# Graph layers on one core: the order of the first loads, earlier searches, first logits inside layer 0, and one product for q and k

## The chip, the cores and the metric

The kernel runs on one core of a Trainium2 chip. The time is the device time of one execution in microseconds; for the kernel before it is the median of 3 runs, 1922.41 us (1921.39 to 1923.52). The profile is of one more execution, of 1922.35 us, with a span of 1920.6 us from its first instruction to its last.

Engines are named as in the profile: PE is TensorE (PEld its weight loads), DVE is VectorE, ACT is ScalarE, POOL is GpSimd, SP is SyncE. An fp32 matmul appears as two PE instructions. [...] DMAs are issued by SP, ACT and POOL.

## What is computed

x has 3327 rows of 256. Layer 0 is a graph attention over a sparse adjacency (3327 x 3327, a few ones in a row) with a gated update; layer 1 makes two propagation steps with a top-p attention over all rows. Each has a residual and a layer norm. Cut to what matters here:

```python
# layer 0
Wh = h @ W
src, dst = Wh @ a[:F], Wh @ a[F:]
e = leaky_relu(src + dst.T, 0.2)
att = softmax(where(adj > 0, e, NEG_INF), axis=1)
h_prime = att @ Wh
gi = h_prime @ w_ih.T + b_ih ; gh = h @ w_hh.T + b_hh
... # r, z, n of a gated unit, then layernorm
# layer 1, for each of two steps
q = Xa @ W1.T @ W2.T
k = Xa @ W3.T
probs = softmax(q @ k.T)
A = probs, kept to the largest that make up 0.9 of a row, normalised
Xf = R @ Xf          # R: (S + identity) over its row sums
Xa = A @ Xa
Z = Z + Xf @ U1[n].T + Xa @ U2[n].T
```

In this program S is the adjacency of layer 0, so that R needs the same neighbour lists. A row without neighbours has the mean of Wh as h_prime; in the table whx this mean is row N.

## The kernel before

**Tiles.** Rows go in 26 tiles of 128 (the last has 127). `HALF` is 1664, the columns of 13 tiles, and `LC` is 416, a quarter of it. kT keeps the keys of the first half on partitions 0 to 63 and those of the second on 64 to 127, and qT has the queries twice, on both halves, so that a product with 64 partitions can take either half of the columns.

**Set-up.** `Shared.__init__` (L514) loads W3, W1 and W2, makes wq = W1 W2 on PE in a pool of its own ("once", released afterwards), and wk; both are doubled in width to fill 128 columns. `Layer0.__init__` (L626) then loads x in pieces on SP (`load_rows`, L635), and on ACT's queue W, its transpose WT, a, the biases, whh and wih. The bias is split into three bf16 parts by DVE (L659 to L661), each of which ACT's queue moves into a row of `bias16` (L662), through one buffer. The three adjacency buffers `ad` are cleared in their borders by POOL (L668, L669).

**Layer 0.** `run` (L978) writes the order out by hand for PE, ACT, DVE and POOL.
- `weights` (L705) multiplies WT by a into two more columns of W.
- `project(t)` (L718): transposes x (L723), multiplies by W (L728), copies into a tile w (L732, three buffers), and ACT issues the write of w to the table whx in DRAM (L735, through `move_rows`, L91). POOL keeps the two added columns in `ds`.
- `column_sums` (L739), and `totals` (L741): column mean of Wh and the largest dst, written to whx as row N; it also fills the columns BOUND, SC and SC3 of `tell`.
- `neighbours(t)` (L783) finds the ones of adjacency tile t: four FIND_INDEX8 (L788), then sorting of the keys, and the load of tile t + 3 into the buffer that came free. It takes five calls.
- `tile(t)` (L804) is a generator with some 43 phases: membership (pst, y, mem, pe, ei), the row numbers (edge, L877), five indirect gathers from whx by POOL (L586, from phase 13), scores (L893 to L895), weights m (L906), acc (L912), gates (L920 to L941), update and layer norm (to L970), x1_rows written, and from phase 39 `Shared.qk` (L592): two transposes, four products (L607: two chunks for q, two for k), a copy to qT (L612) and one to kT (L615).

`advance` makes one phase: one call of the search (`find`), a new tile at every sixth phase, and one phase of each open tile. It is called once per projection from t = EARLY = 17 on; `find` alone from t = 11. After the last projection comes `totals`, then `advance` until all is done.

**Layer 1.** An item is one tile of one step. Per item: logits (`chunk`, L1106: a product of 64 x 416, L1112, and a copy, L1115) into one of two rows `l`; `list_1` (eights per group, L1128), `exp` (L1198), `list_2`, `exp_list`, `list_3`, `mask` (L1234) on DVE and ACT; `fetch` (gathers, L586, and membership tiles, L1271, on POOL); `propagate` (L1279); and `product`: 26 transposes (L1312), copies (L1314) and products (L1328). `run` (L1671) begins with the logits of items 0 and 1, all eight pairs, then the list of item 0, and in the loop makes the logits two items ahead. In step 0 `rest` makes q and k of the next step (`qk` again). At the change of step the last chunk of the first two items is made late (L1752 to L1755), since it needs the last tiles.

Of the kernel before, what the change touches and what calls it, by code (L numbers as in the profile page):

```python
# [16 lines left out]
P = 128  # L17
# [33 lines left out]

EVERY = 6

EARLY = 17
# [456 lines left out]
class Shared:  # L511


    def __init__(self, tc, ctx, W1T, W2T, W3T):  # L514
# [3 lines left out]
        dram = ctx.enter_context(tc.tile_pool(name="dram", bufs=1, space=bass.MemoryType.DRAM))  # L518
        self.ident = keep.tile([P, P], F32, name="ident")
# [3 lines left out]
        self.x1 = keep.tile([P, NT, D], F32, name="x1")  # L523

        self.wq = keep.tile([P, DC, 2 * DA], F32, name="wq")
        self.wk = keep.tile([P, DC, 2 * DA], F32, name="wk")
        for k in range(2):
            nc.scalar.dma_start(self.wk[:, :, k * DA : (k + 1) * DA], W3T.rearrange("(c p) d -> p c d", p=P))
        with ExitStack() as wctx:
            once = wctx.enter_context(tc.tile_pool(name="once", bufs=1))  # L530
            ps = wctx.enter_context(tc.tile_pool(name="onceps", bufs=1, space=PSUM))
            w1 = once.tile([P, DC, DA], F32, name="w1")
            nc.scalar.dma_start(w1, W1T.rearrange("(c p) d -> p c d", p=P))
            w2 = once.tile([DA, DA], F32, name="w2")
            nc.scalar.dma_start(w2, W2T)
            pt = ps.tile([DA, DC * P], F32, name="ptw")
            for c in range(DC):
                nc.tensor.transpose(pt[:, c * P : (c + 1) * P], w1[:, c, :], self.ident)
            w1t = once.tile([DA, DC * P], F32, name="w1t")
            nc.vector.tensor_copy(w1t, pt)  # L540
            pw = ps.tile([P, DC, DA], F32, name="pww")
            for c in range(DC):
                nc.tensor.matmul(pw[:, c, :], w1t[:, c * P : (c + 1) * P], w2, start=True, stop=True)
            for k in range(2):
                nc.vector.tensor_copy(self.wq[:, :, k * DA : (k + 1) * DA], pw)
# [36 lines left out]

    def gather(self, dst, table, t, parts=range(EB)):
# [8 lines left out]
    def qk(self, ps, work, n, t, src, apart=None):  # L592
# [12 lines left out]
        for k, w in enumerate((self.wq, self.wk)):  # L605
            for c in range(DC):
                nc.tensor.matmul(  # L607
                    pq[:, k * P : k * P + r], w[:, c, :], xt[:, c, :r], start=(c == 0), stop=(c == DC - 1)
                )
        if apart:  # L610
            yield
        nc.scalar.copy(self.qT[:, cols(t)], pq[:, :r])  # L612
        h = t * P // HALF
        on = slice(h * DA, (h + 1) * DA)
        nc.scalar.copy(self.kT[on, n, t * P - h * HALF : t * P - h * HALF + r], pq[on, P : P + r])  # L615
# [3 lines left out]
class Layer0:  # L619
# [3 lines left out]
    DST, SRC, ONE, WH = D, D + 1, D + 2, D + 3  # L623
    FIRST, ROW, SC, BOUND, SC3 = MAXDEG, MAXDEG + 1, MAXDEG + 2, MAXDEG + 3, MAXDEG + 4

    def __init__(self, sh, ctx, x, adj, W, WT, a, wihT, whhT, b_ih, b_hh):  # L626
# [7 lines left out]

        load_rows(nc, sh.x1, x, (0, 5, 15, NT - 1))  # L635
# [10 lines left out]
        nc.scalar.dma_start(bi, b_ih.unsqueeze(0))  # L646
        self.whh = keep.tile([P, DC, 3 * D], F32, name="whh")
        nc.scalar.dma_start(self.whh, whhT.rearrange("(c p) d -> p c d", p=P))
# [8 lines left out]
        for k in range(3):  # L657
            part = self.work.tile([1, 4 * D], BF16, tag="part", name=f"part{k}", bufs=1)
            nc.vector.tensor_copy(part, bias)  # L659
            if k < 2:  # L660
                nc.vector.tensor_tensor(bias, bias, part, ALU.subtract)  # L661
            nc.scalar.dma_start(self.bias[k : k + 1, :], part)  # L662
        self.xT = keep.tile([P, DC, N], F32, name="xT")

        self.ad = []
# [1179 lines left out]
```

## Time and profile before

| stage | from to (us) | what carries it |
|---|---|---|
| head: loads, projections | 0 to 87.1 (first gather from whx) | DMA share 0.20 to 1.10 by stretch, PE and ACT with gaps |
| layer 0, with searches | 87.1 to 319.0 | DVE 198.9, PE 185.8, POOL 173.3 of 231.9 us busy |
| layer 0, without | 319.0 to 436.3 (last kT copy) | PE 102.0, POOL 77.8, DVE 51.4 of 117.3 us busy |
| first items | 436.3 to 464.2 | logits of items 0 and 1, list, mask |
| step 0 | 464.2 to 1046 | 22.3 us per tile |
| change of step | 1046 to 1066 | late chunk, list, mask |
| step 1 and end | 1066 to 1920.6 | 21.8 us per tile, then the output |

```profile
PE 1683.6 (88%) x8229; PEld 1243.7 (65%) x8229; DVE 1368.4 (71%) x4291; ACT 902.3 (47%) x2006; POOL 1214.3 (63%) x1891
PE   4578889888999999999998899999999998997844
DVE  2778888434555555565553999999999987988771
PEclk9778999996999999999998899999999999999977
DMA  7666663212111111111111111111111121212110
```

The first line is the busy time of each engine with its share of the span and its instructions; the others divide the span into 40 equal slices (48 us each), a digit being the busy share in tenths. PEclk is the granted clock of PE. The profile's execution of 1922.35 us is within the runs' range, and its span is 1.75 us shorter than its time.

In the tables by stage each row has the stretch and its length, then for each engine the busy time and the number of instructions, then the granted clock, the DMA engines' busy share and GB/s. In a chain of waits each row has start, length and what was waited for: an engine with its line, a DMA, or "issue", in which nothing shown was waited for.

### The profile page before, as it was taken

To read this page: it belongs to the slowest core of one execution; us is meant where nothing else is said; L and a number is where in the kernel's file an instruction comes from. 1 tells how busy PE (TensorE), PEld (TensorE's weight loads), DVE (VectorE), ACT (ScalarE), POOL (GpSimd) and SP (SyncE) were. 2 spreads that over 40 slices of the span, in tenths; PEclk is the share of its full clock that TensorE was granted. 3 is DMA by queue.
4 is the path that set the end of the run, shared out by engine and by line. 5 is a ranking of instruction groups with operands and counts; after the bars stand their busy time and mean duration, and the time that the engine had idled before them with its cause. 6 is when DMAs were issued, how large, how long until landed. Compare 5 with 4: busy or idle time off the path is not lost.

```text
span 1920.6 us, 27507 instructions
## 1 busy us (share of the span) xinstructions
PE 1683.6 (88%) x8229; PEld 1243.7 (65%) x8229; DVE 1368.4 (71%) x4291; ACT 902.3 (47%) x2006; POOL 1214.3 (63%) x1891
## 2 busy tenths in 40 slices
PE   4578889888999999999998899999999998997844
PEld 3345556555777777777775677777777676676733
DVE  2778888434555555565553999999999987988771
ACT  1334445444555555555554455555555454334332
POOL 0277777846656666666664655666556574699993
PEclk9778999996999999999998899999999999999977
DMA  7666663212111111111111111111111121212110
GB/s 248 216 224 204 238 208 99 67 45 77 42 39 44 48 45 39 39 39 42 46 36 39 42 44 49 55 49 47 45 50 54 44 56 31 69 50 83 50 36 20
DMA packets 84192, 143.99 MB, mean 75 GB/s; under 512 B 15546, under 2 KB 57268, under 8 KB 84035
## 3 DMA queue, kind: packets, MB, share of 16 engines
q1 hardware_dynamic: 52272, 78.38, 12.4%
q0 software_dynamic: 20288, 53.27, 10.5%
q10 hardware_dynamic: 11474, 10.49, 1.7%
q8 instruction: 68, 1.11, 0.2%
q14 instruction: 90, 0.73, 0.1%
HBM read 117.84 MB, written 24.35 MB: 74 GB/s over the span
## 4 chain that ended last, share of the span: by engine, by line
PE 39%; DVE 36%; POOL 9%; DMA 5%; ACT 5%; issue 5%; ACTq 0%; POOLq 0%; DVEq 0%
PE pav L1328 17%; PE pl L1112 6%; DVE l L1248 6%; DVE cand L1128 5%; DVE p L1234 5%; DVE cand L1148 4%; PE pxf L1279 3%; PE pt L1312 3%; DVE lst L1146 3%; DMA g<-whx,edge 3%; PE pq L607 2%; POOL g L586 2%; DVE at L788 2%; PE prz L937 2%; PE pavh L1328 1%
## 5 line engine op out<-in xcount | busy, mean ns | idle before, releaser
L1328 PE MATMUL pav<-xa,at 128*128 128x256 f32 (+2 forms) x1352 | 329.8, 389 | 7.4 <-ACT at L1314 7.4
L1328 PE MATMUL pav<-x,at 128*128 128x256 f32 (+2 forms) x1352 | 327.6, 387 | 7.3 <-ACT at L1314 7.3
L1314 ACT COPY at<-pt 128x512 f32<-128x512 f32 (+2 forms) x364 | 191.8, 541 | 289.3 <-PE pt L1312 289.1
L1328 PEld LDWEIGHTS pav<-xa,at 128*128 128x128 f32 (+2 forms) x1352 | 245.6, 191 | 85.4 <-ACT at L1314 42.3
L1328 PEld LDWEIGHTS pav<-x,at 128*128 128x128 f32 (+2 forms) x1352 | 245.8, 191 | 72.2 <-ACT at L1314 29.6
L1128 DVE MAX8 cand<-l 128x8 f32<-128x208 f32 (+5 forms) x936 | 243.3, 336 | 53.6 <-ACT l L1115 53.6
L1115 ACT COPY l<-pl 128x416 f32<-128x416 f32 (+2 forms) x416 | 189.3, 506 | 194.3 <-PE pl L1112 194.3
L586 POOL DMA_INDIRECT g<-xf_rows,edge x130 | 135.8, 1045 | 166.6 <-PE pxf L1279 132.4
L586 POOL DMA_INDIRECT g<-x_rows,edge x130 | 136.2, 1047 | 129.6 <-PE ptq L599 96.8
L1112 PE MATMUL pl<-kT,qT 64*128 64x416 f32 (+1 forms) x832 | 214.2, 581 | 3.3 <-ACT l L1115 1.7
L1312 PE MATMUL pt<-ident,p 128*128 128x128 f32 (+1 forms) x1352 | 200.9, 275 | 15.6 <-DVE p L1234 15.6
L1312 PEld LDWEIGHTS pt<-ident,p 128*128 128x128 f32 (+1 forms) x1352 | 169.1, 144 | 51.9 <-PE pxf L1279 16.9
L1234 DVE SCALAR_TENSOR_TENSOR p<-l,t,p 128x3327 f32<-128x3327 f32 (+1 forms) x52 | 191.3, 3679 | 1.2 <-issue 0.2
L1218 DVE TENSOR_TENSOR_SCAN before<-e 128x40 f32<-128x40 f32 (+3 forms) x52 | 14.3, 275 | 230.5 <-ACT e L1211 230.5
L1198 ACT ACTIVATE p<-l,pay 128x1664 f32<-128x1664 f32 (+1 forms) x104 | 175.2, 1685 | 0.4 <-DVE pay L1190 0.4
L586 POOL DMA_INDIRECT g<-whx,edge x130 | 138.0, 1061 | 46.2 <-issue 30.5
L1271 POOL TENSOR_SCALAR m<-col,erow 128x128 f32<-128x128 f32 x260 | 153.1, 602 | 14.5 <-PE pxf L1279 8.1
L1279 PEld LDWEIGHTS pxf<-g,m 128*128 128x128 f32 (+1 forms) x520 | 99.7, 200 | 57.4 <-issue 39.9
L1279 PE MATMUL pxf<-g,m 128*128 128x256 f32 (+1 forms) x520 | 133.9, 407 | 3.1 <-DVE base L1426 3.1
L1146 DVE MAX8 lst<-cand 128x8 f32<-128x160 f32 (+3 forms) x364 | 114.5, 315 | 9.0
L788 DVE FIND_INDEX8 at<-ones,ad 128x8 uint32<-128x840 f32 (+1 forms) x104 | 106.4, 1026 | 0.0
L1112 PEld LDWEIGHTS pl<-kT,qT 64*128 64x128 f32 (+1 forms) x832 | 68.2, 190 | 45.2 <-issue 26.1
(372 smaller groups left out, 3007.8 us busy)
## 6 DMA issues: line engine op xcount, KB each, us to landing
ad<-in_adj_dram SPq DMA_DIRECT2D x25, 1248.0 KB, 6.4
ad<-in_adj_dram SPq DMA_DIRECT2D x25, 415.5 KB, 6.5
xf_rows<-xf SPq DMA_DIRECT2D x50, 128.0 KB, 1.7
xa_rows<-xa SPq DMA_DIRECT2D x50, 128.0 KB, 1.7
xfs<-xf_rows SPq DMA_DIRECT2D x50, 128.0 KB, 2.1
whx<-w ACTq DMA_DIRECT2D x25, 129.5 KB, 2.9
x_rows<-x ACTq DMA_DIRECT2D x25, 128.0 KB, 2.6
xf<-xf_rows SPq DMA_DIRECT2D x25, 128.0 KB, 2.0
```

The costliest lines, as they stand in the source:

```text
L586: self.nc.gpsimd.indirect_dma_start(out=dst[:, b, :], out_offset=None, in_=table[:, :], in_offset=bass.IndirectOffsetOnAxis(ap=self.edge[: ...
L1112: nc.tensor.matmul(pl[:r, :w], q[on], self.sh.kT[on, n, s : s + w], start=True, stop=True)
L1115: nc.scalar.copy(l[:r, h * HALF + s : h * HALF + s + w], pl[:r, :w])
L1128: self.nc.vector.max(cand[:r, g * 8 : g * 8 + 8], src[:r, g * group : min(N, (g + 1) * group)])
L1146: nc.vector.max(lst[:r, k : k + 8], cand[:r])
L1198: self.nc.scalar.activation(v.p[: v.r, on], v.l[: v.r, on], AF.Exp, bias=v.nmax[: v.r], accum_out=v.sums[: v.r, h : h + 1])
L1234: nc.vector.scalar_tensor_tensor(v.p[:r], v.l[:r, :N], v.t[:r], v.p[:r], ALU.is_ge, ALU.mult, accum_out=sA[:r])
L1271: nc.gpsimd.tensor_scalar(v.m[:, b, :], sh.col1, sh.erow[:, v.at, b : b + 1], None, ALU.is_equal)
L1279: nc.tensor.matmul(acc[:r, :D], v.m[:, b, :r], v.g[:, b, :], start=(b == 0), stop=(b == EB - 1))
L1312: nc.tensor.transpose(pt[: rows(j), j - j0, :r], v.p[:r, cols(j)], self.ident[:r, :r])
L1314: nc.scalar.copy(at[:, :full, :r], pt[:, :full, :r])
L1328: nc.tensor.matmul(v.acc[: v.r, :D], at[:k, j - 4 * g, : v.r], V[:k, j, :], start=(j == 0), stop=(j == NT - 1))
```

## The change

1. Order of the loads: x is loaded first, in pieces of 3, 6, 8 and 8 tiles, in `Shared`; W3, W1 and W2 after the biases; whh and wih only after projection 6. wq is made within the projections (at t = 8 and 10) from work tiles; no pool is released before layer 0. The bias parts have a buffer each and are moved by POOL's queue.
2. `EARLY` is 13 instead of 17, and the searches begin at t = 2 instead of 11. The tile w gets six buffers with the column of ones set once. The column sums are multiplied as they come, and `tell` is filled in two parts without the bound: BOUND goes, and each tile computes its own from src and the maximum (`most`).
3. The three adjacency buffers are shared arrays: once all searches are done, `first_logits` fills arrays 0 and 1 with the logits of step 0's first two tiles, chunk by chunk as their keys are finished (columns 0 to 3199), and the eights of item 0. Layer 1 uses these arrays as `l` and the third as one of its two p rows; it makes only the last 127 columns itself.
4. `qk`: the weights stand as k, q, k side by side, and one product of 128 columns gives both. qT is written by two copies (64 partitions each, one of them from the other half), kT by one.
5. At the change of step more columns of the two first items are made early.

```diff
-EARLY = 17
+EARLY = 13
+LATE = (NT - 1) * P - HALF
+FIRST_CHUNKS = [[(h, s, LC) for h in range(2)] for s in range(0, HALF - LC, LC)] + [
+    [(0, HALF - LC, LC), (1, HALF - LC, LATE - HALF + LC)]
+]
 class Shared:
+        load_rows(nc, self.x1, x, (0, 3, 9, 17, NT - 1))
...
+        self.arrays = [keep.tile([P, SEG * (SW + 8)], F32, name=f"array{k}") for k in range(3)]
+        self.cand = keep.tile([P, -(-N // GROUP[0]) * 8], F32, name="cand0")
+        self.wkqk = keep.tile([P, DC, 3 * DA], F32, name="wkqk")
...
+    def load_weights(self, work):
+        for k in (0, 2):
+            nc.scalar.dma_start(self.wkqk[:, :, k * DA : (k + 1) * DA], W3T.rearrange("(c p) d -> p c d", p=P))
...
     def qk(self, ps, work, n, t, src, apart=None):
-        for k, w in enumerate((self.wq, self.wk)):
-            for c in range(DC):
-                nc.tensor.matmul(
-                    pq[:, k * P : k * P + r], w[:, c, :], xt[:, c, :r], start=(c == 0), stop=(c == DC - 1)
-                )
+        h = t * P // HALF
+        on, other = slice(h * DA, (h + 1) * DA), slice((1 - h) * DA, (2 - h) * DA)
+        for c in range(DC):
+            nc.tensor.matmul(
+                pq[:, :r], self.wkqk[:, c, h * DA : h * DA + P], xt[:, c, :r], start=(c == 0), stop=(c == DC - 1)
+            )
-        nc.scalar.copy(self.qT[:, cols(t)], pq[:, :r])
+        for half in (on, other):
+            nc.scalar.copy(self.qT[half, cols(t)], pq[other, :r])
 class Layer0:
-            part = self.work.tile([1, 4 * D], BF16, tag="part", name=f"part{k}", bufs=1)
+            part = parts[:, k, :]
-            nc.scalar.dma_start(self.bias[k : k + 1, :], part)
+            nc.gpsimd.dma_start(self.bias[k : k + 1, :], part)
...
-            ad = keep.tile([P, SEG, SW + 8], F32, name=f"ad{k}")
+            ad = sh.arrays[k].rearrange("p (g c) -> p g c", g=SEG)
+        self.table = [keep.tile([P, self.WH], F32, name=f"table{k}") for k in range(6)]
...
+        most = self.small("most", f"most{t}", EB)
+        nc.gpsimd.tensor_scalar(most, src, self.dmax, None, ALU.add)
...
+        nc.vector.scalar_tensor_tensor(most, most, ALPHA, most, ALU.mult, ALU.max)
-        nc.vector.tensor_tensor(e, e, ei[:, :, self.BOUND], ALU.subtract)
+        nc.vector.tensor_tensor(e, e, most, ALU.subtract)
+    def first_logits(self):
+        while not self.searched:
+            yield
+        for chunks in FIRST_CHUNKS:
+            while self.done * P < chunks[-1][0] * HALF + chunks[-1][1] + chunks[-1][2]:
+                yield
+            for i in range(2):
...
+                    nc.tensor.matmul(
+                        pl[:, :w], sh.qT[half, cols(i)], sh.kT[half, 0, s : s + w], start=True, stop=True
+                    )
+                yield
+                for pl, (h, s, w) in zip(pls, chunks):
+                    nc.scalar.copy(sh.arrays[i][:, h * HALF + s : h * HALF + s + w], pl[:, :w])
+                yield
+                if i == 0:
...
+                            nc.vector.max(sh.cand[:, at : at + 8], sh.arrays[0][:, c : c + GROUP[0]])
+                    yield
     def run(self):
-        cuts = (0, 7, 14, 20, NT)
+        cuts = (0, 8, 16, 23, NT)
...
+                if t == 6:
+                    for w, src in zip((self.whh, self.wih), self.gates):
+                        nc.scalar.dma_start(w, src.rearrange("(c p) d -> p c d", p=P))
+                if t in (8, 10):
+                    next(qk_weights)
...
                 if t >= EARLY:
                     advance()
-                elif t >= EARLY - 6:
+                elif t >= 2:
                     find()
 class Layer1:
+            late, cut = [(1, LATE)], HALF + LATE
             for i in range(2):
                 self.item(i)
-                for pair in self.chunks():
-                    self.some_logits(i, pair)
+                self.some_logits(i, late)
             self.fetch(0)
-            self.list_1(0)
+            self.list_1(0, cut // GROUP[0] * GROUP[0], N)
...
-                        self.list_1(i + 1, 0, 9 * GROUP[1])
+                        done = [(cut - k * P) // GROUP[1] * GROUP[1] for k in (1, 0)]
+                        self.list_1(i + 1, 0, done[0])
+                        slot(6, self.some_logits, i + 1, [(1, LATE - P)], cut)
+                        slot(6, self.list_1, i + 1, *done)
```

## The prediction

> **What bounds the kernel now.** I read the page's row of slices, then the table by stage (busy time of each engine in a stretch, granted clock, DMA share, GB/s), and then the chain of waits inside each stage that the diff touches. Three stages matter, and each has a different limit.
>
> Table by stage, columns PE, PEld, DVE, ACT, POOL busy with counts, then clock, DMA share, GB/s:
>
> ```profile
> 24.00:30.00 6.00, 5.96 (x22) 4.83 (x23) 0.39 (x1) 0.90 (x3) 0.00 (x0) 1.00 1.04 412
> ...
> 36.00:42.00 6.00, 4.45 (x12) 3.48 (x13) 0.00 (x0) 2.32 (x7) 0.64 (x6) 0.53 0.20 67
> 42.00:48.00 6.00, 6.00 (x28) 4.75 (x28) 4.03 (x5) 3.09 (x9) 1.08 (x10) 0.90 0.27 90
> 48.00:54.00 6.00, 5.66 (x30) 4.37 (x29) 1.34 (x1) 3.39 (x10) 0.96 (x8) 1.00 0.31 100
> ...
> 60.00:66.00 6.00, 1.16 (x7) 0.79 (x6) 5.81 (x15) 0.37 (x1) 0.12 (x2) 0.80 1.03 351
> ```
>
> Chain of waits over the head (start, us, what):
>
> ```profile
> 12.17 8.51 DMA WT_sb<-in_WT_dram
> 20.70 8.89 DMA bias<-part
> 29.61 0.69 DVE part L659
> 30.33 4.60 DMA bias<-part
> ...
> 56.75 8.72 DMA whx<-w
> ...
> 71.67 6.26 DMA whx<-w
> ```
>
> **The head (0 to 87.1 us) is waits, not work.** The first matmul on W waits for WT and a until 21.8; then ACT, which also issues the bias rows' DMAs, stands until 35.7, and with it the projections. From 36 to 54 the DMA engines are at 0.20 to 0.31, because the fourth adjacency load can't start before the first search ends at 56.7. After that they are full, and two writes of whx take 8.7 and 6.3 us, with only three w buffers behind them. The first gather of layer 0 comes at 87.10.
>
> **Layer 0's body (87.1 to 436.3)** has two parts: with searches (to 319.0) DVE is busy 198.9 of 231.9 us; after 380, PE 43.2 of 45.0.
>
> **Layer 0 to layer 1, and step 0.** Chain of waits:
>
> ```profile
> 436.39 1.81 PE pl L1112 x4
> 438.20 0.49 ACT l L1115
> ...
> 452.82 1.77 PE pl L1112 x3
> 454.61 0.43 ACT l L1115
> 455.46 1.53 issue
> 457.00 1.85 ACT p L1198 x3
> ...
> 460.50 3.62 DVE p L1234 x2
> 464.25 1.94 PE pt L1312 x8
> ```
>
> Eight pairs of logits go PE, ACT, PE, ACT, 2.35 us a pair, before the first exp. In step 0 the products start every 22.3 us, and PE is busy 22.0 of them:
>
> ```profile
> 552.30:574.60 22.30, 22.00 (x116) 16.76 (x115) 12.59 (x44) 12.35 (x26) 14.13 (x16) 1.00 0.15 42
> ```
>
> Step 1 (21.8 us a tile) is not touched, nor is the tail.
>
> **1. Head.** W, WT and a are now first on ACT's queue, and no released pool stands before them (W's issue waited until 11.73 for that). But nine ACT DMAs precede the first copy, and the trace shows an issue waiting for a landing several DMAs back (xf_rows<-zero at 5.15, bi at 5.83). I put ACT's first projection at 12.5 us (between 9 and 16) against 26. The bias rows leave ACT for POOL: three issues of about 1.05 us each (nearest row, POOL's indirect gathers), where POOL is idle. Behind them in POOL's order stand the array memsets, and before these the adjacency loads can't be issued; before, POOL reached them at 11.76, so this costs the loads 0 to 4 us. Projections 0 to 12: three cold ones at 2.1 us, ten at 1.5 (row: 1.1 to 1.3 between 44 and 51, and some contention), to 34. Projections 13 to 25 run with the tile pipeline: before, nine took 76.4 - 57.9 = 18.5 us, about 7 of them stall; 13 x 1.4 = 18.2 plus 5 of stall (six buffers instead of three) gives 57, and I add 4 because more adjacency loads now fall here: 61. From the last w (79.26) to the mean row's issue (83.16) are 3.9 us, with 1.86 of PE and six DVE instructions leading to `tell`. Most of the column sum is now accumulated on the way and `tell` no longer waits for the maximum: about 2.5, then some 2.3 until the row has landed. First gather at 66 against 87.10: **-21**, ends -11 and -28. What is late next is this row, since with EARLY = 13 the gather is the first phase after `totals`.
>
> Here a rule speaks against the change. The Trainium skill (DMA: Bandwidth & Descriptors, "Issuing engines are not separate DMA queues") says that DMAs from all issuers share 16 engines and interleave, and the same page puts HBM's share per core at about 358 GB/s. Row first: 412 GB/s at 24 to 30. Until gather 0 there are 3.4 MB of x, 2.3 of weights, 3.4 of whx and five adjacency tiles (8.5): 17.6 MB. By the row that is 43 us, by the rule 49; both need about 6 more, since the first 12 us moved only 2.3 MB. So 49 or 55, under my 61: the head comes close to DMA-bound, so DVE may wait at the early searches. DVE's queue then holds column sums and `w1t`, for which PE waits at t = 9 and 10. That case is rival B.
>
> **2. Layer 0's body.** (a) Search calls done before the first gather: 6 + 13 = 19 before, 11 + 13 = 24 after. A phase takes 231.9/111 = 2.09 us with a search and 117.3/69 = 1.70 without: 5 x 0.39 = **-2**. (b) q and k in one product: 4 instead of 8 PE instructions a tile; in the chain the eight take 0.89 to 1.09 us, so 0.55 is gained where PE is the limit, some 8 tiles: **-4.4**. (c) First logits: 16 products, in pairs at 0.90 us (warm rows of step 0). A chunk waits for 17, 20, 23 or 25 finished tiles; the last two pairs fall into the latency chain after 425, where PE idles; six stand in the PE-bound part: **+5.4** (0 if they fill the 0.8 us before L937; 7.2 if none is covered). Their copies (0.5 us) fit on ACT, 19 of 45 busy; their eights on DVE, 18 of 45. (d) `most`: one DVE instruction (0.17, as L894) in some 18 DVE-bound tiles: **+3**. Its POOL instruction (0.21, as L886) is behind the fifth gather and ahead of the masks; I count it at nothing, +4 if POOL is the limit. (e) ACT's third copy, 0.26 a tile: nothing. No row shows a copy from partitions 64 to 127 into 0 to 63; I take the 0.26 of L615. At several us it would use up the slack (ACT idle 9.9 us a tile in step 0); below 0.26 it would change nothing. Sum **+2**, ends -5 and +9.
>
> **3. Layer 0 to 1.** After: two pieces of 127 columns, a copy, one MAX8, the reductions (together some 2 us), exp 3.6, list 1.6, mask 3.7: the mask is done at 447. Late next is the propagation, which stands ahead of the transposes on PE: its fifth gather was issued at 444.35 and landed at 447.97, held by x_rows and by POOL's 1.3 us a gather, neither of them changed. Then pxf, 4.63 us cold: transposes at 452.6 instead of 464.25, **-11.7**, ends -7 and -14.
>
> The second rule: TensorE: Matmul & The Clock Gate ("Why this matters for your kernels") warns of PE gaps above about 3 us, which put the clock back to half. The change removes 18 us of logits and leaves such a gap. By the rule alone the first product would run cold for some 3.4 us more, about +2. But the row shows clock 0.50 from 436.4 to 454.9 although PE was busy 16.8 of 18.5 us, and 0.52 at 464 to 470: there is no warmth to lose. I take 0.
>
> **4. Step 0.** The eight pq instructions stand at 1.09 us in the chain of every tile, four at 0.55: 25 tiles x 0.545 = **-13.6**. ACT's extra copy is covered by its 9.9 us of idle time. Ends -14 and -9 (if the copy delays the next `at`).
>
> **5. Step 0 to 1.** The late piece shrinks from 415 to 127 columns (PE -0.5, copy -0.25, two MAX8 -0.5), pq -0.55, third copy +0.26; 576 columns more earlier: +0.6. **-0.9**.
>
> Sum: -21 + 2 - 11.7 - 13.6 - 0.9 = -45.2. From the profiled execution's 1922.35 (span 1920.6; the median of the runs shown is 1922.41) that gives **1877**.
>
> **The rivals.**
> A, the sum above: 1877, chance 0.58, own range 1868 to 1886.
> B, the head becomes DMA- or issue-bound, gather 0 at 78: for it, DMA share 1.03 with PE idle 4.8 of 6 us at 60 to 66, and ACT's nine DMAs; against, the empty stretch 36 to 54. -9 in place of -21: 1889, chance 0.23.
> C, the head goes through without these stalls and the logits fill gaps: gather 0 at 59 and -3 in the body: 1865, chance 0.12. For it: 49 us by bytes.
> D, slower. The early searches keep adjacency loads in flight through the whole projection; each write of whx waits behind them, and ACT, which issues them in order, stands. To pass 1926 the head must lose 49 us against A: gather 0 at 115, 3.8 us per projection. With six buffers this decides when a write lands after 6 x 3.8 = 23 us. Against: 8.7 is the longest in the chain, under a DMA share of 1.03. Chance 0.03.
> E, the change does not do what it says, as the first logits start too late (the last chunk waits for tile 24) and run after layer 0, and the head is as in B: 1889 + 7 = 1896, chance 0.04.
>
> Low end 1863, high end 1894 leave out D, most of E and part of C. About 0.2% (3.8 us) can be told from no change. Faster 0.95, same 0.02 (D stopping halfway), slower 0.03.
>
> **What would show it.** First gather from whx at 59 to 72; DMA share above 0.5 between 30 and 54; no ACT wait for a bias DMA; four pq instructions a tile and step 0 at 21.75 us; first transposes of step 0 some 16 us after the last kT copy of layer 0, with PE waiting for gathers and not for the mask. I am wrong if the step-0 period stays at 22.3, if gather 0 is later than 80, or if the time from gather 0 to the last kT copy (349 us) moves by over 9.

## The result, and the profile after

The changed kernel takes 1890.9 us (median of 4 runs, 1890.23 to 1894.84) against 1921.9 for the kernel before beside it. The ratio is 0.9843, with a 95% interval of 0.9826 to 0.9860: 31 us less, where 45 had been forecast. The profiled execution is the longest of the four, 1894.84 us with a span of 1893.1.

Set out by the stages of the prediction, in the two profiled executions (us). "Step 0" runs from the first transposes of its first item to the propagation of its last, the "change of step" from there to the propagation of the first item of step 1:

| stage | before | after | difference | predicted (ends) |
|---|---|---|---|---|
| head, to the first gather from whx | 87.10 | 70.65 | -16.45 | -21 (-28, -11) |
| layer 0's body, to the last kT copy | 349.2 | 361.6 | +12.3 | +2 (-5, +9) |
| last kT copy to first transposes of step 0 | 27.9 | 13.4 | -14.6 | -11.7 (-14, -7) |
| step 0 | 556.1 | 544.3 | -11.8 | -13.6 (-14, -9) |
| change of step | 39.0 | 37.5 | -1.5 | -0.9 |
| step 1 and output | 861.2 | 865.7 | +4.4 | 0 |
| span | 1920.6 | 1893.1 | -27.5 | -45.2 |

Four of the five changed stages went the way forecast and at about the size. Layer 0's body takes 12 us more, and the end 4 more in code that the change doesn't touch. The profile is of one execution of each kernel; heads of equal code come out 1.8 us apart in it (first gather at 70.25 to 72.02 us in the changed kernel and in experiments 1, 3 and 4), so smaller differences between two heads say little.

From the page of the changed kernel, the busy line and the 40 slices of 47 us:

```profile
PE 1662.6 (88%) x8035; PEld 1218.2 (64%) x8035; DVE 1371.5 (72%) x4318; ACT 918.7 (49%) x2063; POOL 1222.8 (65%) x1900
PE   6578778987999999999996999999999998988844
DVE  6789886436556665556654999999999897978771
POOL 1477778837766666666654566556666574699993
PEclk9789889997999999999997999999999998999977
```

PE has 194 instructions less, POOL 8.5 us more work. DVE's first three digits, 6 7 8 where they were 2 7 7, are the early searches. In the tenth slice, between layer 0 and step 0, PE is at 7 with clock 7, where it was at 8 with clock 6: the logits are gone from there. POOL's row is at 7 and 8 through most of layer 0; nothing in it says that POOL sets the pace in the later part of that stage, yet it does.

**The head.** Its table by stage (stretch and length, busy PE, PEld, DVE, ACT, POOL with counts, clock, DMA share, GB/s):

```profile
12.00:24.00 12.00, 11.93 (x52) 9.01 (x51) 5.89 (x16) 5.51 (x16) 3.76 (x17) 1.00 0.92 291
24.00:60.00 36.00, 25.52 (x120) 17.33 (x121) 31.60 (x83) 12.31 (x34) 5.12 (x28) 0.95 1.04 390
60.00:66.00 6.00, 5.15 (x16) 2.40 (x14) 3.32 (x14) 1.77 (x7) 0.60 (x4) 0.72 0.85 265
```

and its chain of waits (start, us, what):

```profile
12.94 2.09 PE pw L751 x4
...
20.49 9.25 DMA whx<-table
29.76 10.02 DMA array<-in_adj_dram
...
40.28 10.62 DMA array<-in_adj_dram
...
53.96 6.46 DMA array<-in_adj_dram
...
64.17 1.08 PE pw L751 x4
...
67.97 1.79 DMA whx<-table
```

The empty stretch of before is gone. From 24 to 60 us the DMA engines are at 1.04 without a break, and four DMAs waited for make up 36.4 of the 40 us from 20.5 to 60.4 in the chain; PE is busy 25.5 of 36. The head now waits for transfers.

**The end of layer 0**, chain of waits of the changed kernel:

```profile
417.21 0.95 PE first L1021 x4
418.16 0.66 ACT array L1026 x2
...
425.96 0.52 ACT array L1026
426.52 0.69 PE ptq L620 x2
427.20 1.68 PE first L1021 x2
428.90 1.32 PE first L1021 x2
430.23 1.16 PE pq L630 x4
```

The first logits stand on the chain: PE makes them, then the next transposes wait until ACT has copied them out, and the last pair (3.0 us for four instructions that took 0.95 before) runs ahead of the product that makes the last tile's own q and k.

**The first transposes of step 0**, timeline of the changed kernel (start, us, engine, line, output<-input, and in brackets the idle time before and what ended it):

```profile
439.41 2.93 PE L1361 MATMUL pxf<-g,m 128*128 128x256 f32 x6 [5.93 <-DVE out L1238]
440.27 3.67 DVE L1316 SCALAR_TENSOR_TENSOR array<-array,t,array 128x3327 f32<-128x3327 f32 x1
...
444.46 1.28 PE L1361 MATMUL pxf<-g,m 128*128 128x256 f32 x4 [2.12 <-POOL m L1353]
...
445.57 1.78 PE L1394 MATMUL pt<-ident,array 128*128 128x128 f32 x8
```

The mask on DVE is done at 443.94, the propagation at 445.74, and its last wait is for POOL's m (forecast: for the gathers). As forecast, the propagation is what is late next, not the mask. **In step 0** the eight pq instructions of a tile have become four, in the chain of waits of before and of after:

```profile
715.46 1.09 PE pq L607 x8
```

```profile
691.23 0.64 PE pq L630 x4
```

and a tile takes 21.84 us in place of 22.29, of which PE is busy 21.6.

### The profile page after: what moved, and what is told of

It reads as the page before. It is cut to its first block, busy times and chain, and to the rows that moved or that the text cites. A ratio compares the mean times of both kernels' runs of the same rounds, so it can differ in the third digit from the quotient of the medians.

```text
span 1893.1 us, 27173 instructions
## 1 busy us (share of the span) xinstructions
PE 1662.6 (88%) x8035; PEld 1218.2 (64%) x8035; DVE 1371.5 (72%) x4318; ACT 918.7 (49%) x2063; POOL 1222.8 (65%) x1900
## 4 chain that ended last, share of the span: by engine, by line
PE 38%; DVE 33%; POOL 12%; ACT 6%; DMA 6%; issue 4%; ACTq 0%; POOLq 0%; DVEq 0%; SPq 0%
PE pav L1410 18%; DVE array L1330 6%; PE pl L1192 5%; DVE cand L1208 4%; PE pxf L1361 4%; PE pt L1394 4%; DVE cand L1228 3%; DMA g<-whx,edge 3%; POOL g L607 3%; DVE lst L1226 3%; DVE p L1316 2%; DVE array L1316 2%; DVE at L812 2%; ACT at L1396 1%; DMA array<-in_adj_dram 1%
## 5 line engine op out<-in xcount | busy, mean ns | idle before, releaser
L1208 DVE MAX8 cand<-array 128x8 f32<-128x167 f32 (+5 forms) x921 | 238.8, 336 | 46.9 <-ACT array L1195 46.9
L1195 ACT COPY array<-pl 128x416 f32<-128x416 f32 (+4 forms) x405 | 182.9, 502 | 183.6 <-PE pl L1192 183.5
L1192 PE MATMUL pl<-kT,qT 64*128 64x416 f32 (+4 forms) x810 | 197.6, 561 | 1.8 <-ACT kT L637 1.8
L1300 DVE TENSOR_TENSOR_SCAN before<-e 128x40 f32<-128x40 f32 (+3 forms) x52 | 14.3, 274 | 216.4 <-ACT e L1293 216.4
L1353 POOL TENSOR_SCALAR m<-col,erow 128x128 f32<-128x128 f32 x260 | 159.6, 628 | 10.0 <-PE pxf L1361 8.0
L1394 PE MATMUL pt<-ident,array 128*128 128x128 f32 (+1 forms) x676 | 101.5, 277 | 6.2 <-DVE array L1316 6.2
L812 DVE FIND_INDEX8 at<-ones,array 128x8 uint32<-128x840 f32 (+1 forms) x104 | 106.5, 1026 | 0.0
L1394 PE MATMUL pt<-ident,p 128*128 128x128 f32 (+2 forms) x676 | 100.4, 275 | 4.5 <-DVE p L1316 4.5
L1394 PEld LDWEIGHTS pt<-ident,array 128*128 128x128 f32 (+1 forms) x676 | 85.2, 145 | 24.7 <-PE pxf L1361 8.2
L1394 PEld LDWEIGHTS pt<-ident,p 128*128 128x128 f32 (+2 forms) x676 | 84.6, 144 | 22.0 <-PE pxf L1361 8.6
L965 PE MATMUL prz<-wih,hT 128*128 128x512 f32 (+1 forms) x104 | 68.1, 790 | 34.3 <-ACT hT L963 34.3
```

The source lines that it names most:

```text
L812: nc.vector.max_index(at[:r, g, :], self.ones8[:r], ad[:r, g, :])
L1192: nc.tensor.matmul(pl[:r, :w], q[on], self.sh.kT[on, n, s : s + w], start=True, stop=True)
L1195: nc.scalar.copy(l[:r, h * HALF + s : h * HALF + s + w], pl[:r, :w])
L1208: self.nc.vector.max(cand[:r, g * 8 : g * 8 + 8], src[:r, g * group : min(N, (g + 1) * group)])
L1353: nc.gpsimd.tensor_scalar(v.m[:, b, :], sh.col1, sh.erow[:, v.at, b : b + 1], None, ALU.is_equal)
L1394: nc.tensor.transpose(pt[: rows(j), j - j0, :r], v.p[:r, cols(j)], self.ident[:r, :r])
```

## The experiments

Three things had to be explained: where 12 us went in layer 0, what holds the head, and what each part of the change is worth. Three theories stood against each other for layer 0: the place of the first logits in PE's order costs (called R in the expectations); POOL sets the pace, so that what PE or DVE save is worth nothing and what POOL is given costs (Q; at first P, any cause other than the logits); or DVE does with searches and PE without, as I had read before. For the head: its bytes (called D), or the number of w buffers.

POOL's work of one tile late in layer 0, after the searches, from the timeline of the changed kernel:

```profile
300.25 1.13 POOL L607 DMA_INDIRECT g<-whx,edge  x1 [0.52 <-PE acc L940]
301.68 0.99 POOL L607 DMA_INDIRECT g<-whx,edge  x1 [0.30 <-issue]
...
306.49 1.92 POOL L934 TENSOR_SCALAR m<-col,erow,we 128x128 f32<-128x128 f32 x2
308.57 1.10 POOL L607 DMA_INDIRECT g<-whx,edge  x1 [0.16 <-issue]
...
310.02 0.32 POOL L913 TENSOR_SCALAR most<-src,dmax 128x5 f32<-128x5 f32 x1
...
312.45 1.13 POOL L607 DMA_INDIRECT g<-whx,edge  x1 [0.52 <-DVE e L920]
```

From one first gather to the next are 12.2 us without a gap above 0.52. The 0.30 between two gathers counts as idle in the busy share, but the profile shows nothing that POOL waits for in it. From the first gather of tile 5 to that of tile 25 the period was 12.49 us before and 12.78 after, of which POOL was busy 9.69 and 9.92 and stood 1.18 and 1.19 in such gaps. That leaves some 1.6 us a tile in which POOL stood for other reasons. What they were can be read from POOL's waits before (engine and line, what it waited for, us in total, times, longest), first from tile 5 to tile 18, with searches, then from there to tile 25, without:

```profile
POOL g L586 <- issue: 14.6, 53, 0.5
POOL mv L965 <- DVE which L868: 12.1, 12, 2.0
```

```profile
POOL g L586 <- issue: 9.1, 31, 0.5
POOL g L586 <- PE acc L912: 2.6, 5, 0.5
```

With searches POOL waits for DVE, once in nearly every tile; without them it waits for nothing longer than 0.5 us.

All ratios are against the kernel before, run beside the experiment; a step of 0.001 is 1.9 us. The change itself has 0.9843 [0.9826, 0.9860]. Edits are against the changed kernel unless said otherwise.

**1. No first logits in layer 0.** Layer 1 makes all pairs itself.

```diff
-        logits = self.first_logits()
...
-            next(logits, None)
...
-            for _ in logits:
-                pass
...
-                self.some_logits(i, late)
+                for pair in self.chunks():
+                    self.some_logits(i, pair)
...
-            self.list_1(0, cut // GROUP[0] * GROUP[0], N)
+            self.list_1(0)
```

> The changed kernel, but all logits of the first two items are made in layer 1 again; nothing in layer 0 is asked of PE, ACT or DVE for them. Theory R (ring): the first logits take two of two buffers of the tag tr, so that the next transposes wait for ACT's copies; together with PE's own time this cost layer 0 some 12 us (6.5 before the last acc, 5.9 after it) of the 14.6 us gained at the start of layer 1. Then this kernel takes 1893 to 1895 (2 to 4 more than 1890.9), and first gather to last kT copy falls from 361.6 to about 350. Rival P (layer 0 grew for another reason, such as POOL's added instruction or the shared DMA): 361.6 stays within 3 us and the time rises by 12 or more, to about 1903.

Measured: 1897.5 us, ratio 0.9871 [0.9855, 0.9887], so 5.4 us slower than with the change (the two intervals just overlap), and above the 1893 to 1895 expected. Body 352.9 instead of 361.6; from the last kT copy to the transposes 27.9 instead of 13.4. The logits cost 8.7 in layer 0 and bring 14.5 behind it: about 6 net, most of what they bring is given back.

**2. Two products for q and k**, all else as changed.

```diff
-                pq[:, :r], self.wkqk[:, c, h * DA : h * DA + P], xt[:, c, :r], start=(c == 0), stop=(c == DC - 1)
+        for k, w in enumerate((self.wq, self.wk)):
...
+                    pq[:, k * P : k * P + r], w[:, c, :], xt[:, c, :r], start=(c == 0), stop=(c == DC - 1)
...
-        for half in (on, other):
-            nc.scalar.copy(self.qT[half, cols(t)], pq[other, :r])
+        nc.scalar.copy(self.qT[:, cols(t)], pq[:, :r])
```

> The changed kernel with q and k by two products of 128 columns and two copies, as before. Theory: the product is worth 0.45 us a tile in step 0 (its chain fell from 1.09 to 0.64), 25 tiles, so 11 us there, and up to 4 in layer 0, where PE is the limit in some 8 tiles: 1902 to 1906, step-0 period 22.29. Rival: step 0 became faster through something else (the arrays, the order of copies): period stays near 21.84 and the time within 3 us of 1890.9.

Measured: 1905.61 us, 0.9911 [0.9896, 0.9926], 13 us more. The step-0 period is 22.286 again, so step 0 loses 11 us (555.3 against 544.3). The body is 361.3 against 361.6: in layer 0 the one product brings nothing.

**3. First logits only in the gap of the phases.** The first three pairs are made only at the fifth phase of six, where PE is thought to have room.

```diff
+                while self.phase % EVERY != 4 and chunks is not FIRST_CHUNKS[-1]:
+                    yield
...
+            self.phase = phase
```

> The changed kernel, but the products of the first three chunks of the first logits are issued only at the phase that follows the gate products (phase 4 of 6), so that their copies are done long before the next transposes need the buffers. Theory R: the waits of ptq and ph for the copies vanish in layer 0's tail, three times about 2 us: 1883 to 1886; a period with logits takes 10.7 instead of 12.9 or 14.9. Rival P: no change, 1889 to 1892.

Measured: 1891.56 us, 0.9838 [0.9824, 0.9851], not to be told from the change, where 1883 to 1886 had been expected. The body is 4.8 shorter (356.8) but 2.8 of that comes back behind it, where the transposes come at 16.2 rather than 13.4. A better place in PE's order shortens layer 0, but the start of step 0 hardly moves (444.99 instead of 445.57).

**4. The last pair of chunks made in layer 1.**

```diff
-        for chunks in FIRST_CHUNKS:
+        for chunks in FIRST_CHUNKS[:-1]:
...
-                self.some_logits(i, late)
+                self.some_logits(i, self.chunks()[-1])
...
-            self.list_1(0, cut // GROUP[0] * GROUP[0], N)
+            self.list_1(0, HALF - LC, HALF)
+            self.list_1(0, 2 * HALF - LC, N)
```

> The changed kernel with the last of the four chunk pairs made in layer 1 (416 and 415 columns in place of 127), so that nothing of the logits stands in the chain from the last acc to the last kT copy. Theory R: that chain falls from 26.3 to about 20.5 us (5.8 less); the first item's list comes some 2.5 us later after the last kT copy, part of it hidden by the gathers: 1886 to 1889. Rival P: the chain stays near 26 and the time rises by 2, to 1893.

Measured: 1889.86 us, 0.9823 [0.9810, 0.9837]: no difference that can be told. In the trace the stretch from the last acc to the last kT copy falls from 26.3 to 23.6 (20.3 without any first logits, 20.5 before), so the last pair accounts for about half of what this stretch grew by, and 0.6 of it returns behind it.

**5. Without `most`.** The scores are shifted by the largest dst rather than by each row's own bound; the softmax is the same.

```diff
-        nc.gpsimd.tensor_scalar(most, src, self.dmax, None, ALU.add)
...
-        nc.vector.scalar_tensor_tensor(most, most, ALPHA, most, ALU.mult, ALU.max)
-        nc.vector.tensor_tensor(e, e, most, ALU.subtract)
+        nc.vector.tensor_scalar(e, e, self.dmax, None, ALU.subtract)
```

> The changed kernel without most: the score has the maximum of dst subtracted (the softmax of a row is the same whatever constant the row subtracts), so POOL loses its added 128x5 instruction and DVE one of two. Theory Q: POOL, with five gathers, two masks and a dozen small instructions a tile, is the limit of layer 0 once the searches are over, and with the added instruction its cycle is 12.2 us; then the time from the last search to the last acc falls from 111.8 by some 4 us, first gather to last search by 0 to 3, and the whole by 3 to 7 us against 1890.9 (the ratio to before by 0.002 to 0.004 below 0.9843). Rival: PE and the logits set the tail; then less than 1 us is gained there.

Measured: 1885.68 us, 0.9806 [0.9792, 0.9820], some 7 us less; in the trace the body is 4.4 shorter, and 3.9 of that after the searches have ended, where DVE has plenty of idle time. With searches the period of a tile stays (13.28 us with `most`, 13.25 without), after them it falls from 12.03 to 11.64. So it is the 0.32 us on POOL (0.42 with its gap), not the instruction on DVE, that costs. What the ratio has beyond these 4.4 us is less than the two intervals leave open.

**6. Searches from t = 7** instead of 2.

```diff
-                elif t >= 2:
+                elif t >= 7:
```

> The changed kernel with the searches begun at t = 7 instead of 2 in the projections, so that about one adjacency tile (1.7 MB) less is loaded before the last projection. Theory D: from 24 to 60 us the head is bound by the DMA engines, where prefetched adjacency loads share them with the writes of whx: the last projection comes about 4 us earlier (61 instead of 64.9) and the first gather at 67; in the body five phases more have a search, +2 us; in all 1887 to 1891. Rival: DVE or PE sets the pace of the projections: last projection within 1 us of 64.9, and the time 2 us longer.

Measured: 1887.19 us, 0.9805 [0.9793, 0.9818], 7 us less than the change. Fourteen adjacency DMAs start before the last projection instead of sixteen, but the last projection comes at 64.3 (64.9 after; 61 expected if the bytes alone held it) and the first gather at 70.13. The DMA engines now have a hole:

```profile
42.00:48.00 6.00, 5.48 (x26) 3.35 (x24) 5.83 (x12) 2.55 (x7) 1.66 (x9) 0.96 0.81 243
```

(the changed kernel has 1.05 and 410 GB/s there). So without those loads the DMA engines have time over, and the projections still come no sooner; the first gather moves by less than heads of equal code differ. The early searches bring nothing: in the changed kernel the searches end 6.7 us earlier than here (294.0 against 300.7), yet its body is 6.0 longer. Half of the 6.0 stands in one tile. In the changed kernel 17.3 us pass from the first gather of tile 15 to that of tile 16, here 14.3; in the chain of waits of the changed kernel stands

```profile
254.82 9.36 DMA g<-whx,edge
```

the last gather of tile 14, while the adjacency's loads keep the DMA engines busy (share 1.05 from 260 to 265 us); DVE waits 5.5 us for it. The other gathers that stand in this chain take 4 to 7 us up to there and 3.4 to 3.7 behind it. The other half of the 6.0 is left open.

**7. Three w buffers** instead of six.

```diff
-        self.table = [keep.tile([P, self.WH], F32, name=f"table{k}") for k in range(6)]
+        self.table = [keep.tile([P, self.WH], F32, name=f"table{k}") for k in range(3)]
```

> The changed kernel with three tiles for the rows of whx instead of six. Theory: with the DMA engines full from 24 to 60 us a write of whx takes up to 9 us to land, so with three buffers projections wait for it: first gather 4 to 10 us later than 70.65, the whole 1895 to 1901. Rival: the lanes of earlier DMAs, not the buffers, hold ACT: within 2 us of 1890.9.

Measured: 1901.51 us (1891.5 to 1907.37), 0.9879 [0.9855, 0.9902], 7 us more, with intervals that just overlap; in the trace the first gather comes at 78.87, 8.2 later, body 360.4. Half of the head's gain hangs on the three more buffers, behind which the projections can go on while a write of whx takes up to 9 us among the adjacency loads.

**8. EARLY = 17**, the value before; searches still from t = 2.

```diff
-EARLY = 13
+EARLY = 17
```

> The changed kernel with the tiles begun at t = 17 instead of 13 (searches still from t = 2). Theory: the projections end 2 to 4 us sooner, since four phases fewer stand between them, but the first gather comes four phases after the totals, about 8 us later: first gather at 75 to 78, the whole 1893 to 1897. Rival: in a DMA-bound head the order of the phases is of no weight: within 2 us of 1890.9.

Measured: 1886.96 us, 0.9812 [0.9800, 0.9825], some 6 us less than the change. The first gather comes at 68.61, earlier and not at 75 to 78 as expected: the last projection comes at 59.6 instead of 64.9, since fewer tile phases stand between projections, and the body is 356.5. Tile 15 takes 14.1 us here, so 3.2 of the body's 5.1 are again that one late gather. Starting tiles at t = 13 costs time on this base.

**9. POOL's second mask on ACT.** Experiment 5, and of the five weights m one more is made by ACT (square and relu, as two already were), one less by POOL.

```diff
-        for k in (3, 4):
+        for k in (2, 3, 4):
             nc.scalar.activation(ms[k], sh.col1, AF.Square, bias=minus[:, k : k + 1])
...
-        for k in (0, 1, 2):
+        for k in (0, 1):
```

> The kernel without most, with one of POOL's two masks per tile (0.8 to 1.0 us) made on ACT, as two others already are. Theory Q: POOL is the limit of layer 0 from the first gather on (gathers come every 12.3 to 13 us with searches or without), so its cycle falls by about 1 us a tile, until PE (9.8 us) or DVE (some 88% busy with searches) takes over: first gather to last acc falls from 330.8 by 8 to 20 us, the ratio to before from 0.9806 to 0.970 to 0.977. Rival: a chain of latencies through several engines sets the pace, which does not shorten when POOL has less to do: within 2 us of the kernel without most.

Measured: 1875.62 us, 0.9751 [0.9737, 0.9765], 10 us less than experiment 5 by the ratios. From the first gather to the last acc it takes 316.5 us against 330.8, -14.3 where 8 to 20 had been expected. POOL's cycle of one tile, timeline of experiment 9:

```profile
280.05 1.12 POOL L607 DMA_INDIRECT g<-whx,edge  x1 [0.52 <-PE pq L630]
...
286.35 0.84 POOL L930 TENSOR_SCALAR m<-col,erow,we 128x128 f32<-128x128 f32 x1
287.36 1.10 POOL L607 DMA_INDIRECT g<-whx,edge  x1 [0.18 <-issue]
288.50 0.21 POOL L910 TENSOR_TENSOR src<-ei 128x5 f32<-128x5 f32 x1
...
290.94 1.12 POOL L607 DMA_INDIRECT g<-whx,edge  x1 [0.52 <-PE acc L936]
```

10.9 us, against 12.2 in the changed kernel and 11.8 without `most`. After the searches each tile lost about what POOL no longer does (11.64 to 10.84 us a tile), although PE, DVE and ACT do the same as before or more: there POOL is the limit. With searches the period fell too, from 13.25 to 12.59, but half of that is tile 15, which takes 13.2 us here and 17.0 in experiment 5.

**10. Experiment 9 with EARLY = 17.**

> The kernel before this one (no most, one mask moved to ACT) with the tiles begun at t = 17, not 13. Theory: as without the mask moved, the last projection comes some 5 us sooner and the first gather 2 us sooner, and four phases fewer are slowed by the full DMA engines: 2 to 6 us less. Rival: the 5 us seen there were chance of the phases' order: within 1.5 us.

Measured: 1876.16 us, 0.9745 [0.9728, 0.9761]; the first gather is 2.6 earlier, the body 2.5 longer. Not told apart from experiment 9: the gain of experiment 8 does not add to it. Part of the reason is in the trace: the late gather of tile 14, which experiment 8 was rid of, is gone in experiment 9 already.

**11. Experiment 10 with the logits in the gap** (the edit of experiment 3).

> The same with the first logits' products only at the phase after the gate products. Theory R, narrowed: with POOL relieved, PE is the limit after the searches, so that the wait of the transposes for the copies of the first logits counts: 2 to 4 us less than the kernel without this. Rival: the copies are covered by other waits: within 1.5 us.

Measured: 1868.44 us (1867.46 to 1871.93), 0.9716 [0.9701, 0.9731], below both kernels. The body falls from 345.6 to 340.3, its last stretch from 26.5 to 23.4. Of these 5.3, 2.0 come back behind the last kT copy (15.2 us to the transposes instead of 13.2), so the trace has 3.3, within the 2 to 4 expected; the ratio has some 5.6, but its interval just overlaps that of experiment 10. In experiment 3 the same edit took 4.8 off the body and gave 2.8 back. So the traces don't show that this edit is worth much more once POOL is relieved; that the order on PE counts only then is a guess that fits the ratios.

**12. The kernel before with the mask on ACT**, and nothing else.

```diff
-        for k in (3, 4):
+        for k in (2, 3, 4):
...
-        for k in (0, 1, 2):
+        for k in (0, 1):
```

> The kernel before the change, with one of POOL's two masks per tile made on ACT and nothing else. Theory Q: POOL set layer 0's pace already there, so first gather to last acc falls from 328.8 by 8 to 14 us and the ratio is 0.9925 to 0.996. Rival: before, DVE (with searches) and PE (without) were the limits, as the prediction read it, and POOL became one only through the change: 0 to 3 us, ratio 0.998 to 1.000.

Measured: 1918.79 us (13 runs), 0.9968 [0.9954, 0.9982], 6 us less, a little short of the range expected. In the trace the first gather to the last acc falls from 328.8 to 319.6, within the 8 to 14 expected. Nearly all of it comes after the searches. The mean period from one tile's first gather to the next one's (us), where the searches end at tile 18 in the kernel before and at 17 in the changed one:

| | with searches, from tile 5 | after them, to tile 25 |
|---|---|---|
| before | 12.93 | 11.67 |
| experiment 12: before, one mask less on POOL | 12.84 | 10.74 |
| changed kernel | 13.28 | 12.03 |
| experiment 5: without `most` | 13.25 | 11.64 |
| experiment 9: that, one mask less on POOL | 12.59 | 10.84 |

After the searches the period falls by what POOL no longer does, here 0.93 us. With them it stays, and what POOL was spared turns up as its wait for DVE, 12.1 us before and here, for the same thirteen tiles,

```profile
POOL mv L965 <- DVE which L868: 20.3, 13, 2.1
```

So in the kernel before POOL set the pace only once the searches were over. With them POOL waits for DVE, and in the chain of waits of before every second or third of these tiles has a gather that takes 6 to 7 us to land among the adjacency loads. No run here takes work off DVE or thins out those loads in the body, so which of the two holds that part is not shown. The profiled execution's tail was 7.4 us longer than that of the kernel before; the last section is about such differences.

## Why the prediction was right or wrong

The whole came out at 1890.9, inside the range but above A's own 1868 to 1886, and beside B's 1889. That is chance: B has its 12 us in a late first gather (78), while here most of what is missing was lost in layer 0.

**1, the head: right, two terms mis-sized.** ACT's early start was right (first W product forecast for 12.5, measured at 12.94), and so was DMA share above 0.5 from 30 to 54. The first thirteen projections were to be done at 34 and were at 38.2; the other thirteen took the 27 us forecast (done at 65.2, for which I had 61), and the first gather came 5.4 later instead of 5. So in the sum the first thirteen were mis-sized: the eighth was done at 23.8, but the next five took 14.4 us instead of 7.5, and in the chain stand there a write of whx of 9.25 us and an adjacency load of 10.02. I had put "some contention" at a fraction of that. The volume behind it was mis-sized too, the 17.6 MB: by the table by stage 255 x 12 + 291 x 12 + 390 x 36 + 265 x 6 = 22.2 MB moved in 66 us. I counted five adjacency tiles; sixteen of their DMAs, eight tiles, were issued by then, because each finished search starts the load three tiles ahead. At 412 GB/s those 22.2 MB take 54 us and with the slow beginning 60; by the 358 GB/s that I had weighed against it 62 and 68. The measured rate was 390 on average over 36 us. The Trainium skill (DMA: Bandwidth & Descriptors, "Measured") puts 358 down to two cores that stream at once and gives 425 for a core alone with 16 MB; this kernel runs on one core, so the rule was the wrong one to take, and the row the better guide. Yet bytes alone are not the limit: with two of these DMAs fewer the first gather does not move beyond what heads of equal code differ by (experiment 6), with three w buffers fewer it comes 8.2 later (experiment 7), and with fewer tile phases between the projections 2.0 earlier (experiment 8; 2.6 in experiment 10). So the picture of rival B, a head full of transfers, came true, but not its 78.

**2, layer 0's body: wrong, and this is the step that failed.** I read "with searches (to 319.0) DVE is busy 198.9 of 231.9 us; after 380, PE 43.2 of 45.0" as the limits, and counted POOL's instruction "at nothing, +4 if POOL is the limit". The first half of that reading agrees with experiment 12, in which POOL with less to do only waits longer for DVE. The second half is wrong: after the searches POOL was the limit, not PE (experiments 5, 9, 12), hidden by a busy share (67.3 us of 81.7 before, PE 72.8) that leaves out its gaps between gathers. The body moved by 12.3 us, over the 9 that the prediction had named as a sign of being wrong. Term by term: without first logits and without `most` the body would be 361.6 - 8.7 - 4.4 = 348.5, against 349.2 before, if the two add up. So
- (a) and (b), forecast at -2 and -4.4, gave together -0.7, with the late gather of tile 14 (some 3 us) in it. The one product saved PE time that nothing waited for (experiment 2); more searches ahead gave nothing (experiment 6).
- (c), forecast at +5.4, was 8.7. The sentence that "the last two pairs fall into the latency chain after 425, where PE idles" is the mistake: PE idles there because it is in a chain, and what is put into a chain lengthens it. The granted clock is 0.50 from 425 to 432, and ACT's copies stand behind. About half of the 6 us lost there are the last pair's (experiment 4); the other 2.6 stand before the last acc.
- (d), forecast at +3 on DVE with searches, was 4.4, on POOL and after them.
- (e), ACT's third copy, cost nothing, as forecast.

**3, layer 0 to 1: right, at the end of its range.** The transposes come 13.4 us after the last kT copy instead of 27.9. Propagation was late next, as forecast; but its fifth gather, which I had taken as unchanged, goes out 5.5 us after the last kT copy and not 8.0 as before, so that it ends about 3 us earlier than I had put it. PE stands idle for 5.93 us before the propagation, and the granted clock is 0.50 from 436 to 442; but it was 0.50 in this place before too, and the eight transposes took 1.78 us here, 1.94 before. So nothing was lost, and 0 was right. The rule that I weighed against it, of the Trainium skill (TensorE: Matmul & The Clock Gate, "Why this matters for your kernels"), would have added about 2.

**4, step 0: right, one term mis-sized.** 0.446 us a tile instead of 0.545: four instructions take 0.64, not half of 1.09. By my estimate from the two rows each instruction costs 0.11 and the group some 0.19 once, which halving leaves.

**5, change of step**: -1.5 against -0.9.

**The stages that weren't touched** gave +4.4. The code there is the same, and other executions of it differ as much: see the last section. Without the 4.4 the profiled execution would be at 1890.4, where the other three runs are (1890.23 to 1891.48).

What the change's parts are worth, by the ratios, each give or take some 4 us: one product 13 us, six w buffers 7, first logits 5, `most` -7, searches from t = 2 -7, EARLY = 13 about -6; the last is 0 on the base of experiment 9. They don't sum to 31, and the last two share the late gather of tile 14. The order of the loads, with the bias rows on POOL's queue, was not undone by itself; that it is the part left over, most of it in the head, is not shown.

## What to carry to other kernels

Find the engine that sets the pace from its period, not from its busy share: list one tile's instructions of each engine from the first to the same one of the next tile, and see which list has no long gap that something else ends. Do it for each part of a stage: here the answer changed when the searches ended. The gaps of "issue" between indirect gathers, 0.30 us each here, belong to that engine's own time. Then take a piece of work off the engine: if the period falls by as much, it was the limit; if the piece turns into a wait, follow what is waited for. Time in which an engine idles inside a chain of dependences is not room for more work on that engine; put such work in front of the chain, or behind it.

## What the runs showed of the hardware

**The same code took up to 7 us more or less at the end.** From item 47 to the end no kernel differs, yet this stretch took 394.8 us in the profile of before, 398.6 after, 394.6 in experiment 5 and 402.2 in experiment 12. The granted clock goes with it: tables by stage for the same two items, of before,

```profile
1600.50:1625.50 25.00, 23.34 (x115) 17.54 (x113) 19.15 (x59) 13.08 (x27) 5.17 (x13) 0.95 0.09 27
1625.50:1660.00 34.50, 31.68 (x157) 24.54 (x157) 32.59 (x47) 13.68 (x29) 26.98 (x12) 1.00 0.26 66
```

and of experiment 12,

```profile
1594.70:1622.70 28.00, 26.08 (x114) 19.29 (x112) 19.21 (x59) 13.04 (x26) 5.20 (x13) 0.84 0.08 25
1622.70:1660.00 37.30, 35.12 (x153) 25.56 (x151) 34.64 (x56) 14.21 (x29) 26.98 (x12) 0.86 0.24 56
```

Nearly the same instructions, the same DVE and ACT time in the first row, and PE 2.7 us longer at clock 0.84. What decides the clock there is open.

**A copy between partition halves was not dearer.** ACT's two copies into qT of 64 x 128, one straight and one from the other 64 partitions, took 0.256 to 0.263 us each over all 104.

**Gathers landed later among the adjacency loads.** In the chain of waits of the changed kernel's layer 0 the gathers from whx take 5.2 to 9.4 us from 120 to 260 us, while adjacency tiles are loaded, and 3.4 to 3.7 after 280.
